# A four-layer graph network on one core: node counts fetched and compared inside the first dense layer, half of one stage's norms ended by ScalarE

## The chip, the cores and the metric

One Trainium2 chip, one core. The metric is the device time of one execution in microseconds (us). Before the change it is 3164.61 us, the median of 21 runs (3158.17 to 3174.01).

The engines are named as in the profile: PE (TensorE matmuls), PEld (its weight loads), DVE (VectorE), ACT (ScalarE), POOL (GpSimd) and SP (SyncE, which here only issues DMAs). Each engine works through its own list of instructions in order; an instruction that waits holds up all behind it on that engine. DMAs are issued from SP, ACT or POOL; indirect ones (gathers by a list of row numbers) from POOL.

## What is computed

A graph of 6250 nodes with 128 features and 106250 edges (100000 of two directions and one loop per node), sorted by destination `dst`. Four layers follow one another, each ended by a residual and a LayerNorm:

```python
x = layernorm(x + L0(x, edge_attr_128, src, dst, ...))   # sum of edge features by node, two dense products
x = layernorm(x + L1(x, edge_index, ...))                 # sum of x[src] by dst, two dense products, two batch norms
x = layernorm(x + L2(x, edge_index, ...))                 # twice: mean of x[src] by dst, dense products
x = layernorm(x + L3(x, edge_index, edge_attr_16, ...))   # attention over the edges of a node
...
def _layernorm(x, axis=-1, eps=1e-05):
    m = jnp.mean(x, axis=axis, keepdims=True)
    v = jnp.var(x, axis=axis, keepdims=True)
    return (x - m) / jnp.sqrt(v + eps)
```

L2 needs for every node the number of its edges (`cnt`, for the mean), and L3 the place of a node's first and last edge in the sorted list. Both follow from `upto`: for each node, how many edges have a destination up to it.

## The kernel before, in words

Nodes are worked on in 50 blocks of 125 (`PB`, `NB5`), and blocks in 13 `CHUNKS` of four (the last has two).

**Dense layers.** The sum of `x[src]` by `dst` in L1 and both sums of L2 are made by `neighbours`. For the first 5000 nodes it is a dense product with a matrix of edge counts, which the L0 stage has written to DRAM (`matrix`): 10 sums of 500 nodes, each from 10 pieces of 5 blocks. A piece (`piece`, L843, 640 KB, issued by SP) feeds 15 matmuls (L846), for each of its five blocks three: the rows of x stand in `arena` as three bf16 parts, `hi`, `mid` and `lo`, that `split` makes (ACT L377, DVE L378, ACT L379, DVE L380). So a dense layer has 100 pieces and 1500 of these matmuls. For the other nodes the edges are gathered: 16 quads of up to 12 rows-tiles (`row`, L801, one indirect DMA of POOL for 128 edges each, 183 in all, buffers for two quads), each summed by 12 small matmuls with one-hot matrices (`both`, L341), copied by ACT (L343), transposed by PE (L345) and added by DVE (L348). Below, "the first quad" to "the sixteenth" are these. A sum that is done goes through `take` (DVE L910 in L1), and the work of `then` or `late` follows a few pieces later on PE (in L1: `hidden`, L903).

**What goes on beside the first dense layer.** After each piece `each(i)` takes one step of two generators. `logits` fetches the 16 edge features (`eat`, L692, L694, cleared by L691, seven buffers) and multiplies them on DVE (L684, L685). `counting` finds for each node block the edge `n0` from which its 128 destinations are to be read: POOL writes a row of numbers (L543), DVE compares it seven times (L545, L547), PE sums (L537), DVE makes `n0` and `n0i` (L431, L432, L540), five blocks a step, eleven steps (`i % 7 == 1`).

**After the first dense layer.** `counted` fetches for all 50 blocks at once the 128 destinations from `n0i` on (`edges_from`, L437, 50 indirect DMAs of POOL into `nd`, 25.6 KB per partition). Then come the two dense products of L1 with batch norm (L903, L941, L945, L946), and the norm stage, chunk by chunk:

- DVE L957, ACT L959, DVE L960: batch norm's scale and shift, relu, residual;
- PE L315: four transposes to nodes (`node_p`, in PSUM);
- one step of `counted` (`degrees.send`): DVE compares the chunk's fetched destinations with the node numbers (L564), sums them (L565) and adds `n0` (L566): `upto`;
- `layernorm`: DVE statistics (L291, L293), ACT square root (L295), DVE reciprocal (L298), and the norm itself, one DVE instruction per block (L300);
- SP stores the chunk to `table` (L271), `split` makes the three parts, PE L308 and ACT L309 go back to features.

After the last chunk two shifted matmuls (L575, L576) give the start of each node, the counts' reciprocal and the last edge (L577 to L580). Then the second dense layer begins: POOL fetches its rows from the stored table, SP its pieces.

The order of the generators says when steps are emitted, but not where they end up: a scheduler orders each engine's instructions by priorities and its own estimate of what is ready, and pools give buffers and with them waits. Memory of a pool that is closed is reused by the next, which then waits until it is free; `nd` is held until the last chunk of the norm stage.

Of the kernel before, what the change touches and what calls it, by code (L numbers as in the profile page):

```python
# [209 lines left out]
def by_windows(ctx: ExitStack, tc: tile.TileContext, a: dict, out: bass.AP, consts, ix):  # L210
# [70 lines left out]
    def layernorm(to, x):  # L281

        for _ in norm_steps(to, x):
            pass

    def norm_steps(to, x):
# [11 lines left out]
        nc.vector.reciprocal(rstd[:PB, :nb], sd[:PB, :nb])  # L298
        for j in range(nb):
            nc.vector.tensor_scalar(to[:, j, :], x[:, j, :], mv[:PB, j, 0:1], rstd[:PB, j:j + 1],  # L300
                                    op0=OP.subtract, op1=OP.mult)
# [248 lines left out]
    def counted(pool):  # L550
# [6 lines left out]
        nd = pool.tile([128, NB5, 128], I32, name="nd")  # L557
        edges_from(a["dst"], n0i[:PB], nd[:PB])
        for blocks in CHUNKS:
            work = yield  # L560
            cs, nb = slice(blocks[0], blocks[-1] + 1), len(blocks)
            up = upto[:PB, 1 + cs.start:1 + cs.stop]
            lt = work.tile([128, 4, F], F32, name="rest")
            nc.vector.tensor_tensor(lt[:PB, :nb], nd[:PB, cs], over(thn[:PB, cs], 128), op=OP.is_lt)  # L564
            nc.vector.tensor_reduce(up, lt[:PB, :nb], AX.X, OP.add)  # L565
            nc.vector.tensor_add(up, up, n0[:PB, cs])  # L566

# [5 lines left out]
        p = (yield).tile([128, 4, F], F32, name="node_p")[:, 0, :]  # L573
        start = p[:PB, 0:NB5]
# [6 lines left out]
        yield  # L581
# [287 lines left out]
    with tc.tile_pool(name="l1", bufs=1) as wp:  # L869
# [37 lines left out]
        with tc.tile_pool(name="l1d", bufs=1) as dp, tc.tile_pool(name="l1e", bufs=7) as two, \  # L907
                tc.tile_pool(name="hps", bufs=4, space=bass.MemoryType.PSUM) as hps:
# [7 lines left out]
            logit, indices = logits(dp, two), counting(dp, hps)  # L916

            def each(i):
                if i % 7 == 1:
                    next(indices, None)  # L920
                if i % 3 == 2:
                    next(logit, None)

            neighbours(None, take, then, tables[0], len(matrix), each)
            for x in (logit, indices):
                for _ in x:
                    pass
        counts = ExitStack()
        degrees = counted(counts.enter_context(tc.tile_pool(name="l1c", bufs=1)))
        next(degrees)  # L930
        with tc.tile_pool(name="l1p", bufs=1) as lp, tc.tile_pool(name="l1w", bufs=2) as work, \
# [4 lines left out]
            for k in range(len(PARTS)):  # L936
# [11 lines left out]
                if k in (2, 4):  # L948
                    next(looped)
        batchnorm(2, s2, b2, g2, be2)  # L950
        with tc.tile_pool(name="l1x", bufs=2) as work, tc.tile_pool(name="zps", bufs=3, space=bass.MemoryType.PSUM) as zps, \
                tc.tile_pool(name="tps", bufs=2, space=bass.MemoryType.PSUM) as tp:
            last = None
            for blocks in CHUNKS:
# [9 lines left out]
                degrees.send(work)  # L964
                layernorm(xn[:PB, b0:b0 + nb, :], z)
# [6 lines left out]
            degrees.send(zps)  # L972
        counts.close()
# [950 lines left out]
```

## Time and profile before

| what | number |
|---|---|
| median of 21 runs | 3164.61 us (3158.17 to 3174.01) |
| the profiled execution | 3168.92 us, its span 3167.1 us |
| busy share of the span | PE 79%, DVE 55%, POOL 53%, PEld 48%, ACT 28% |
| granted PE clock, mean | 0.899 |
| first dense layer, first to last sum | 641.4 to 1006.5 us |
| norm stage of L1, DVE | from 1060.8 to 1139 us |
| first row of the second dense layer, its first and last sum | 1141.2, 1151.2, 1525 us |

The profile is of one execution. For every instruction it has the start, the length, the line of the code and what ended the idle time before it. Groups are written as line, engine, operation, out<-in and count. A view of windows gives the busy time of each engine in a stretch, with the share of full speed at which PE's clock was granted. In the timeline, the bracket behind an instruction says how long its engine had been idle before it and what came last before it went on; "issue" is time in which it waited for nothing that the profile shows.

### The profile page before, as it was taken

Reading aid. Unit: us, or ns where it says so; the run is one execution under the profiler, and the core shown is the slowest. Engines: PE = TensorE matmul, PEld = TensorE weight load, DVE = VectorE, ACT = ScalarE, POOL = GpSimd, SP = SyncE. Lnnn points to the kernel's source line nnn. Section 1 sums busy time; section 2 is a strip of 40 time slices with the busy share of each in tenths; the row PEclk is TensorE's granted clock in tenths of the full one; section 3 lists DMA queues with packets and bytes.
Section 4 is the critical chain, followed back from the end, with each engine's and each line's share of the span. In section 5 each row is a group of like instructions: output and inputs, shape, how many; then the busy total and the mean of one; then the engine's idle time right before and its main releaser. Section 6 shows DMA issues by size and latency. Waiting matters only on the chain.

```text
span 3167.1 us, 42839 instructions
## 1 busy us (share of the span) xinstructions
PE 2511.8 (79%) x14960; PEld 1532.5 (48%) x14960; DVE 1728.5 (55%) x4636; ACT 898.3 (28%) x1661; POOL 1673.9 (53%) x1664
## 2 busy tenths in 40 slices
PE   2788899989999669999999999276666666766665
PEld 1444445634444334545544444165555555655564
DVE  4777874569512850000131112477767777877776
ACT  0688884400001410000210000033323332333332
POOL 5000002078742546665077742577777777777773
PEclk9998889989999779999999999588888888988888
DMA  5799972188773256666376665322222222222221
GB/s 159 228 308 299 301 257 93 46 248 257 228 217 111 69 169 200 198 195 185 88 251 189 212 187 163 79 63 70 69 67 71 66 71 70 71 69 69 70 69 39
DMA packets 335096, 465.22 MB, mean 147 GB/s; under 512 B 45340, under 2 KB 219196, under 8 KB 334275
## 3 DMA queue, kind: packets, MB, share of 16 engines
q1 hardware_dynamic: 251434, 278.98, 29.9%
q0 software_dynamic: 54912, 105.86, 12.4%
q10 hardware_dynamic: 28524, 77.55, 6.7%
q8 instruction: 119, 1.95, 0.3%
q14 instruction: 107, 0.88, 0.1%
HBM read 377.01 MB, written 85.06 MB: 146 GB/s over the span
## 4 chain that ended last, share of the span: by engine, by line
PE 32%; DVE 13%; DMA 8%; issue 6%; POOL 6%; ACT 3%; DVEq 0%; ACTq 0%; POOLq 0%; SPq 0%
PE sums L846 16%; PE o L1203 6%; DMA rows<-x,srca 5%; POOL rows L1093 4%; DVE w L1191 3%; DVE w L1176 2%; ACT w L1193 2%; POOL row L801 2%; PE yp L1021 1%; PE w_p L1181 1%; DMA row<-table,srca 1%; DVE mx L1184 1%; PE fp L1137 1%; PE o L1153 1%; PE both L341 1%
## 5 line engine op out<-in xcount | busy, mean ns | idle before, releaser
L846 PE MATMUL sums<-piece,arena 125*128 125x500 bf16 x4500 | 990.4, 376 | 4.3 <-DMA piece<-edges 4.3
L1093 POOL DMA_INDIRECT rows<-x,srca x831 | 843.5, 1015 | 278.1 <-issue 171.8
L801 POOL DMA_INDIRECT row<-table,srca x549 | 540.8, 985 | 292.6 <-issue 128.2
L846 PEld LDWEIGHTS <-arena 125*128 125x128 bf16 x4500 | 431.2, 97 | 518.0 <-issue 33.2
L1203 PE MATMUL o<-rows,w 128*120 128x132 f32 x2078 | 359.6, 313 | 240.7 <-ACT w L1193 240.7
L1203 PEld LDWEIGHTS o<-rows,w 128*120 128x120 f32 x2078 | 309.4, 211 | 283.7 <-ACT w L1193 283.4
L646 ACT CAST arena<-made 128x1000 bf16<-128x1000 f32 (+1 forms) x260 | 315.9, 1280 | 61.9 <-PE made L644 57.5
L1193 ACT ACTIVATE w<-w 128x720 f32<-128x720 f32 x208 | 167.0, 803 | 438.0 <-DVE w L1191 399.7
L644 PE MATMUL made<-okey,olow 128*128 128x250 bf16 x1000 | 258.1, 400 | 35.2 <-ACT arena L646 17.2
L1181 PE MATMUL w_p<-ident,w 128*120 128x128 f32 x1248 | 200.0, 296 | 23.4 <-DVE w L1176 21.1
L1184 DVE TENSOR_REDUCE mx<-w_p 120x1 f32<-120x768 f32 x208 | 197.7, 951 | 18.8 <-PE w_p L1181 17.8
L343 ACT COPY by_node<-both 128x128 f32<-128x128 f32 (+1 forms) x48 | 12.7, 264 | 684.9 <-PE both L341 627.5
L352 DVE TENSOR_TENSOR onehot<-iota,relg 128x384 f32<-128x384 f32 x118 | 63.8, 545 | 247.1 <-PE both L341 235.4
L1176 DVE TENSOR_TENSOR w<-oh,z 128x720 f32<-128x720 f32 x208 | 187.3, 901 | 8.2 <-PE o L1203 6.6
L717 POOL MEMSET ea<- 128x128 f32 x1 | 0.2, 206 | 357.1 <-DMA ea<-in_edge_attr_dram 357.1
L1191 DVE TENSOR_TENSOR w<-w,both 128x720 f32<-128x720 f32 x208 | 186.8, 898 | 2.8 <-PE both L1188 2.4
L1181 PEld LDWEIGHTS w_p<-ident,w 128*120 128x120 f32 x1248 | 159.4, 150 | 54.2 <-DVE w L1176 23.1
L644 PEld LDWEIGHTS <-olow 128*128 128x128 bf16 x1000 | 109.9, 119 | 155.3 <-issue 69.4
L617 DVE TENSOR_TENSOR okey<-iok,key 128x1000 bf16<-128x1000 bf16 (+1 forms) x260 | 169.9, 653 | 0.0
L348 DVE TENSOR_TENSOR arena<-arena,both 128x32 f32 x183 | 34.2, 187 | 211.4 <-PE both L345 203.2
L1161 DVE TENSOR_TENSOR z<-rows,zed 128x12 f32<-128x12 f32 x208 | 34.4, 165 | 197.0 <-DMA rows<-x,srca 196.7
L341 PE MATMUL sums<-ea,onehot 128*32 128x128 f32 x1662 | 98.6, 335 | 47.6 <-DMA ea<-in_edge_attr_dram 30.4
(287 smaller groups left out, 3362.1 us busy)
## 6 DMA issues: line engine op xcount, KB each, us to landing
piece<-edges SPq DMA_DIRECT2D x300, 625.0 KB
edges<-arena ACTq DMA_DIRECT2D x100, 625.0 KB
ea<-in_edge_attr_dram SPq DMA_DIRECT2D x69, 768.0 KB
loop<-x SPq DMA_DIRECT2D x208, 68.0 KB
rows<-x,srca POOLq DMA_INDIRECT x831
row<-table,srca POOLq DMA_INDIRECT x549
eat<-in_edge_attr_dram POOLq DMA_DIRECT2D x28, 236.0 KB
table<-xn SPq DMA_DIRECT2D x24, 224.0 KB
```

The lines of the kernel that those rows point to most:

```text
L617: nc.vector.tensor_tensor(o[:, :, 0:n], numbers[:, :, 0:n], of.rearrange("p (o g) -> p o g", o=1).to_broadcast([128, m, n]), op=OP.is_equal)
L644: nc.tensor.matmul(p[:, i, 0:NB5 * GD], lhsT=o[:, :, i], rhs=w[:, :, i], start=True, stop=True)
L646: nc.scalar.copy(to, p[:, 0:n, 0:NB5 * GD].rearrange("p i (h d) -> p i h d", d=GD))
L801: nc.gpsimd.indirect_dma_start(out=r[:, j, :], out_offset=None, in_=table, in_offset=bass.IndirectOffsetOnAxis(ap=ix["src"][:, t:t + 1], a ...
L846: nc.tensor.matmul(p, lhsT=xp[:PB, h, i, :], rhs=t[:PB, :, (h - h0) * SC:(h - h0 + 1) * SC], start=(h == 0 and i == 0), stop=(h == NB5 - 1 ...
L1093: nc.gpsimd.indirect_dma_start(out=r[:, j, :], out_offset=None, in_=x3, in_offset=bass.IndirectOffsetOnAxis(ap=ix["src"][:, BT * b + j:BT ...
L1176: nc.vector.tensor_tensor(w, oh.to_broadcast([128, S, H, BW]), z.rearrange("p j (h w) -> p j h w", w=1).to_broadcast([128, S, H, BW]), op= ...
L1181: nc.tensor.transpose(tp[:, j // 3, j % 3 * 128:(j % 3 + 1) * 128], w[:, j, :, :].rearrange("p h w -> p (h w)"), ident)
L1184: nc.vector.tensor_reduce(mx, tp[:, :, 0:384], AX.XY, OP.max)
L1191: nc.vector.tensor_tensor(wf, wf, mb.rearrange("p (j h) w -> p j (h w)", j=1) .to_broadcast([128, S, H * BW]), op=OP.subtract)
L1193: nc.scalar.activation(wf, wf, AF.Exp)
L1203: nc.tensor.matmul(o[:, 0:F + H + 1], lhsT=wf[:, j, :], rhs=rr, start=(j == 0), stop=(j == S - 1))
```

## The change

Two edits.

1. `counted` becomes a generator within the first dense layer. It fetches the destinations for two blocks at a time into one of three small buffers (`nd` of 1 KB per partition) and compares the two blocks before, on DVE, with the result in bf16. `each` steps it twice per piece from piece 72 of 100 on. The fetches are kept in program order among the instructions so marked. `counting` steps every sixth piece instead of every seventh. The end of it, the shifted matmuls and what follows from them, becomes `degrees`, called within the second of the dense products of L1. Nothing of it remains in the norm stage.
2. In the norm stage, two blocks of each chunk get their norm from ACT instead of DVE: `Identity` with scale `rstd` and bias `off` = -mean * rstd, which DVE makes for the chunk in one small instruction.

```diff
     def norm_steps(to, x, by_act=0):
...
         nc.vector.reciprocal(rstd[:PB, :nb], sd[:PB, :nb])
+        if by_act:
+            off = small.tile([128, 4], F32, name="off")
+            nc.vector.scalar_tensor_tensor(off[:PB, :nb], mv[:PB, :nb, 0], -1.0, rstd[:PB, :nb],
+                                           op0=OP.mult, op1=OP.mult)
         for j in range(nb):
+            if j < by_act:
+                nc.scalar.activation(to[:, j, :], x[:, j, :], AF.Identity, bias=off[:PB, j:j + 1],
+                                     scale=rstd[:PB, j:j + 1])
+                continue
             nc.vector.tensor_scalar(to[:, j, :], x[:, j, :], mv[:PB, j, 0:1], rstd[:PB, j:j + 1],
                                     op0=OP.subtract, op1=OP.mult)
...
-    def counted(pool):
+    def counted(pool, work):
...
-        nd = pool.tile([128, NB5, 128], I32, name="nd")
-        edges_from(a["dst"], n0i[:PB], nd[:PB])
-        for blocks in CHUNKS:
-            work = yield
+        found = []
+
+        def compare(blocks, nd):
             cs, nb = slice(blocks[0], blocks[-1] + 1), len(blocks)
             up = upto[:PB, 1 + cs.start:1 + cs.stop]
-            lt = work.tile([128, 4, F], F32, name="rest")
-            nc.vector.tensor_tensor(lt[:PB, :nb], nd[:PB, cs], over(thn[:PB, cs], 128), op=OP.is_lt)
+            lt = pool.tile([128, 2, 128], BF16, name="fewer")
+            nc.vector.tensor_tensor(lt[:PB, :nb], nd[:PB, :nb], over(thn[:PB, cs], 128), op=OP.is_lt)
             nc.vector.tensor_reduce(up, lt[:PB, :nb], AX.X, OP.add)
             nc.vector.tensor_add(up, up, n0[:PB, cs])
+
+        for blocks in [c[i:i + 2] for c in CHUNKS for i in (0, 2) if c[i:]]:
+            nd = work.tile([128, 2, 128], I32, name="nd")
+            for i, b in enumerate(blocks):
+                tc.keep_in_program_order(nc.gpsimd.indirect_dma_start(
+                    out=nd[:PB, i, :], out_offset=None, in_=a["dst"].rearrange("(e o) -> e o", o=1),
+                    in_offset=bass.IndirectOffsetOnAxis(ap=n0i[:PB, b:b + 1], axis=0)))
+            yield
+            found.append((blocks, nd))
+            if len(found) > 1:
+                compare(*found.pop(0))
+        compare(*found.pop(0))
+
+    def degrees(pool, psum):
...
-        p = (yield).tile([128, 4, F], F32, name="node_p")[:, 0, :]
-        start = p[:PB, 0:NB5]
+        start = psum.tile([128, 2 * SC], F32, name="hp2")[:PB, 0:NB5]
...
+                tc.tile_pool(name="l1n", bufs=3) as ndp, \
...
+            finding = counted(dp, ndp)
             def each(i):
-                if i % 7 == 1:
+                if i % 6 == 1:
                     next(indices, None)
                 if i % 3 == 2:
                     next(logit, None)
+                if i >= 72:
+                    next(finding, None)
+                    next(finding, None)
...
-        counts = ExitStack()
-        degrees = counted(counts.enter_context(tc.tile_pool(name="l1c", bufs=1)))
-        next(degrees)
...
+                if k == 6:
+                    degrees(lp, hps)
...
-                degrees.send(work)
-                layernorm(xn[:PB, b0:b0 + nb, :], z)
+                layernorm(xn[:PB, b0:b0 + nb, :], z, 2)
...
-            degrees.send(zps)
-        counts.close()
```

More of the change, by code (lines that the diff above doesn't have):

```diff
@@ L279, in row_over, with layernorm, norm_steps @@
         return x.rearrange("p (b f) -> p b f", b=1).to_broadcast([PB, nb, x.shape[1]])
-    def layernorm(to, x):
-        for _ in norm_steps(to, x):
+    def layernorm(to, x, by_act=0):
+        for _ in norm_steps(to, x, by_act):
             pass
-    def norm_steps(to, x):
+    def norm_steps(to, x, by_act=0):
         nb = x.shape[1]
@@ L580, in counted @@
         nc.vector.tensor_scalar(lasti[:PB], upto[:PB, 1:], -1.0, None, op0=OP.add)
-        yield
     def products():
@@ L922, in each @@
                     next(logit, None)
+                if i >= 72:
+                    next(finding, None)
+                    next(finding, None)
             neighbours(None, take, then, tables[0], len(matrix), each)
-            for x in (logit, indices):
+            for x in (logit, indices, finding):
                 for _ in x:
                     pass
-        counts = ExitStack()
-        degrees = counted(counts.enter_context(tc.tile_pool(name="l1c", bufs=1)))
-        next(degrees)
         with tc.tile_pool(name="l1p", bufs=1) as lp, tc.tile_pool(name="l1w", bufs=2) as work, \
```

## The prediction

> **What bounds the kernel now.** I read the page first (busy shares by slice), then the windows around the change, then the chain of waits from 620 to 1180 us, then POOL's and PE's instructions in order of time. The stages touched are the first dense layer (641 to 1006), the two dense products of L1 (1006 to 1061), the L1 norm stage (1061 to 1138) and the start of the second dense layer (to 1151). The table of windows gives, per stretch, length, then busy us of PE, PEld, DVE, ACT and POOL, the granted PE clock, DMA share and GB/s:
>
> ```profile
> 632.00:870.00 238.00, 218.99 (x1245) 101.90 (x1249) 176.80 (x283) 2.65 (x10) 186.72 (x210) 0.96 0.79 244
> 870.00:1006.00 136.00, 136.00 (x730) 62.74 (x723) 17.85 (x55) 1.58 (x6) 37.79 (x39) 1.00 0.60 185
> 1061.00:1138.00 77.00, 31.62 (x104) 21.05 (x104) 76.02 (x253) 32.63 (x63) 20.96 (x17) 0.51 0.21 54
> 1151.00:1525.00 374.00, 374.00 (x2005) 183.62 (x2004) 35.32 (x107) 27.53 (x60) 230.13 (x226) 1.00 0.66 199
> ```
>
> The dense layers are PE's: it is busy all the time from 870 to 1006 and from 1151 to 1525. The norm stage is DVE's: 76 of 77 us. In 632 to 870 POOL looks free (187 of 238), and is not. Its timeline (start, length, instruction, idle before it) shows that every indirect fetch is followed by 0.30 us in which nothing is waited for:
>
> ```profile
> 858.82 0.94 POOL L801 DMA_INDIRECT row<-table,srca  x1 [0.30 <-issue]
> 860.07 0.94 POOL L801 DMA_INDIRECT row<-table,srca  x1 [0.30 <-issue]
> 861.32 0.99 POOL L801 DMA_INDIRECT row<-table,srca  x1 [0.30 <-DMA row<-table,srca]
> 862.61 1.50 POOL L801 DMA_INDIRECT row<-table,srca  x1 [0.30 <-issue]
> ```
>
> So a row costs POOL 1.25 us. Adding up the gaps beyond that 0.30 from 634 to 880 leaves under 4 us: until about 870 POOL is full. After it POOL waits for free row buffers, and idles from 935.
>
> What moves is this group (min/median/max ns, first and last start), and what it feeds on DVE:
>
> ```profile
> L437 POOL DMA_INDIRECT nd<-in_dst_dram,n0i x50: 1178/1197/2340, 1007.0 to 1083.9; - x50
> L564 DVE TENSOR_TENSOR rest<-nd,node_col x13: 418/685/693, 1038.0 to 1134.8; 125x512 f32<-125x512 int32 x12, 125x256 f32<-125x256 int32 x1
> ```
>
> A fetch costs POOL 1.197 + 0.30 = 1.50 us.
>
> **First dense layer: +40.** The edit asks for the fetches from piece 72 of 100 on, where POOL is idle. But the order in which the changed kernel, as built, hands POOL its instructions puts them earlier: 5 fetches stand ahead of the fourth quad's rows, 8 ahead of the fifth's, 18 ahead of the eighth's, 30 ahead of the ninth's, 35 ahead of the tenth's, 40 ahead of the twelfth's, and only 10 behind the last. POOL works in that order, and PE's order has the quads' matmuls at the same pieces as before, so a late quad stops PE and all sums behind it. In before the twelfth quad's last row is issued by 869.7 and its matmuls run at 891.4 to 892.0:
>
> ```profile
> L341 PE MATMUL both<-row,onehot x24: 272/273/297, 891.4 to 892.0; 128*32 128x128 f32 x24
> ```
>
> 40 x 1.50 = 60.0 us more ahead of it, and landing: in the third layer, where PE does wait for rows, a quad's last matmul starts 1.9 us after its last row's issue ends (1685.1, 1687.0). 869.7 + 60.0 + 1.9 = 931.6 against 892.0: late by 39.6. The ninth quad (817.6 + 45 + 1.9 against 831.0) is late by 33.5 already, the eighth (802.5 + 27 + 1.9 against 814.2) by 17; from the thirteenth on POOL gains on PE (15 us of rows per 17 to 22 us of PE), so 40 stays. Lower end: the 4 us of POOL's idle absorb as much, and contention does not lengthen the fetches: 34. Upper end: rows in this stretch run at up to 1.5 us instead of 0.94 here and there; fetches at 1.6, and waits for DVE: 50. DVE's 25 compares of two blocks (0.42 + 0.42 + 0.15 = 0.99 each, from the 256-wide rows: 24.7 us) lie in its 61 idle us of 632 to 870; but a compare waits in DVE's order for its fetch, with one-hots, L348 and `take` behind it, and a fetch waits for a compare three tiles back. As ordered, the fourth `take` stands behind the thirteenth compare, thus behind POOL's eighth quad and 8 more fetches, and PE's `hidden` of that sum stands ahead of the eighth quad's matmuls: 802.5 + 27 + 13 (8 fetches and a chunk of `eat`) + 2 to land + 5 of DVE's work between puts it near 850, and PE needs 19 us from there to the ninth quad: 869 against 830.4, again 39. Where DVE is full (59 of 60 us in 700 to 760) that cover is gone; this is in the upper end.
>
> **The two products: 0.** One chunk's compare (1.5 us at 1038) leaves DVE, `degrees` comes (four matmuls of 50 columns, 0.9 us on DVE).
>
> **Norm stage: -12.5.** Off DVE: L564, L565 and L566 of 11.5 chunks, which start 0.69 + 0.60 + 0.13 apart: 16.3; two of four L300 of each chunk, 26 x 0.32 = 8.3; the closing L577 to L580, 1.0. On it: `off`, 13 x 0.15 (as L566) = 2.0. DVE's floor is 77 - 23.6: one end is -23.6. The other is 0: two other engines take over. ACT gets 26 norms; nearest rows are its 128x128 copy (L343, 0.26) and the 125x256 cast (0.40): I take 0.35, 9 us, ACT 42, not the bound. PE gets new work: the big `nd` tile gone, the second layer's pieces find room before the stage ends, and PE's order now has about 148 of that layer's 1500 sums among the transposes, some 125 ahead of the last chunk's. A late chunk's transposes stand behind sums that read the split of about two chunks earlier. Priced from before: a chunk's chain from its first statistics to its split took 10.9 us (1125.4 to 1136.3) on a full DVE; less the 1.9 that each of two chunks no longer takes: 7.1; transposes 1.3 and ten sums of 0.211: 10.5 per two chunks, 5.2 per chunk, 65 for 12.5 chunks. 77.5 - 65 = 12.5, between the ends.
>
> **Second dense layer: -25.** The first row is fetched when the last table rows have landed, and PE then waits for rows, not sums:
>
> ```profile
> 1141.21 0.98 POOL L801 DMA_INDIRECT row<-table,srca  x1 [54.68 <-DMA l2wr<-in_L_gnn_W_r_dram]
> ...
> 1150.66 0.63 PE L341 MATMUL both<-row,onehot 128*32 128x128 f32 x2 [2.69 <-DMA row<-table,srca]
> ```
> ```profile
> L341 PE MATMUL both<-row,onehot x24: 272/273/297, 1215.7 to 1216.3; 128*32 128x128 f32 x24
> ```
>
> Counted from that first row, the third quad's matmuls came at +74.5. In the new order the first two quads stand at pieces 11 to 14, and the sums ahead are done in time: the second quad's rows are issued by +30.2, landed by +32.1; then 45 sums (9.5) and the first mean's products (7.5: the 23.3 us between these quads before, less 75 sums) give +49.1. The third quad's rows (by +46.7, landed 48.6) don't delay it. Gain 25.4. From there POOL needs some 19 us a quad, PE 22: nothing is lost again. Ends: -28, and -18 if rows land as late as the 5.6 us at 1145.
>
> **Sum**, on the profiled execution: 3168.92 us with a span of 3167.1 and 1.8 around it. +39.6 + 0 - 12.5 - 25.4 = +1.7. That execution is 4.3 above the median of 21 runs, 3164.61, so I forecast 3166.3, call it 3167: no change. 0.2% (6.3 us) is about what a measurement here can tell from none.
>
> [...] The clock: PE's granted clock was 0.51 in the norm stage and came back some 3 us after its sums ran without gaps (from 1151.2 they started 0.42 apart, later 0.211). [...] Also, half of the norms change from a copy-like form to Identity with pointers. A table load took 1.28 us where Exp and Sqrt alternate after 2046. [...]
>
> **Rivals.**
> - *Slower: the norm stage keeps its length.* At half clock 125 sums take 52 us and 100 transposes 27 (50 x 0.32 + 50 x 0.21, this stage's spacing): 79, no less than 77.5. From about 65 us of PE work on, PE is the bound. For: clock 0.51 now. Against: runs of 6, 12 and 15 sums stand together. Price 12.5: 3179. A table load before each Sqrt and Identity group (26 x 1.28 = 33 on ACT, 75 in all) would give the same; the change would then not do what it says for DVE. With it I count a longer stall of the first layer (50: 3177). 0.36.
> - *Faster: DVE's floor is reached and POOL absorbs its 4 us.* 36 - 23.6 - 25.4 = -13: 3152. For: the as-built order interleaves two to three chunks. Against: the sums between transposes. If the fetches cost PE nothing at all, 3167 - 40 = 3127; the gapless POOL timeline speaks against it (0.04). Together 0.26.
> - *No change*, 0.38.
>
> **Range.** Best ends 34 - 23.6 - 28 = -17.6; worst 50 - 0 - 18 = +32. Both at once are unlikely; 8 in 10: 3150 to 3187. Faster by over 0.2% 0.26, within 0.38, slower 0.36.
>
> **What would show it.** Right: `nd` fetches from about 700 on between rows; PE idle before the eighth and ninth quads' matmuls on `row`, some 35 us together; the last sum of the first layer near 1046; norm stage of 60 to 68 us with PE's sums inside; the third quad of the second layer some 49 us after its first row. Wrong: no such idle in the first layer (much faster), or the norm stage still 77 us long (slower).

## The result and the profile after

The changed kernel takes **3219.07 us** (median of 8 runs, 3212.74 to 3220.76) against 3166.53 (56 runs) for the kernel before: ratio 1.016, 95% interval 1.0148 to 1.0172, that is 52 us slower. The forecast was 3167, with a range up to 3187; the time lies outside it. The profiled execution of the changed kernel took 3216.04 with a span of 3214.2, 47.1 more than before.

By stage, between the same instructions in both traces (L1 is the first dense layer, from its first sum to its last; the products run from there to the last `bnshift`; the norm stage from there to the first row of the second layer; the second layer from that row to the third layer's first sum):

| stage | before | after | difference | forecast |
|---|---|---|---|---|
| L1 | 364.8 | 457.2 | **+92.4** | +39.6 (34 to 50) |
| two products | 54.4 | 54.7 | +0.3 | 0 |
| norm stage | 80.7 | 62.3 | -18.4 | -12.5 (-23.6 to 0) |
| second layer from its first row | 443.7 | 420.6 | -23.1 | -25.4 (-28 to -18) |
| start, third layer, rest | 2223.5 | 2219.4 | -4.1 | 0 |

So the norm stage and the second layer came out inside their bounds and the products at 0.3. The miss is L1, 52.8 us above its term. The windows of the changed kernel, in the columns of the table of windows of before (length, busy us of PE, PEld, DVE, ACT, POOL, granted clock, DMA share, GB/s):

```profile
632.00:870.00 238.00, 171.29 (x909) 78.40 (x913) 155.65 (x271) 1.86 (x7) 183.94 (x199) 0.86 0.66 200
870.00:1098.20 228.20, 202.29 (x1067) 92.72 (x1059) 60.61 (x157) 2.39 (x9) 104.99 (x101) 0.93 0.55 170
1153.00:1215.20 62.20, 54.41 (x260) 29.44 (x261) 56.00 (x203) 42.70 (x92) 0.05 (x1) 0.89 0.48 137
1215.20:1602.40 387.20, 375.79 (x1980) 184.12 (x1979) 41.17 (x117) 33.89 (x70) 236.01 (x233) 0.98 0.61 183
```

From 632 to 870 PE did 909 matmuls where it had done 1245. DVE and POOL were *less* busy than before (156 against 177, 184 against 187) although both had been given work: PE and DVE waited. POOL did not: counted with the 0.30 us behind every indirect fetch, it had some 8 us of other idle time in this stretch (3 before), so that it was as full as the prediction had it. In the norm stage the granted clock is 0.89, not 0.51, and PE has 260 matmuls there instead of 104.

The moved fetches and their compares (min/median/max ns, first and last start):

```profile
L578 POOL DMA_INDIRECT nd<-in_dst_dram,n0i x50: 1178/1199/2055, 698.2 to 1029.0; - x50
```
```profile
L571 DVE TENSOR_TENSOR fewer<-nd,node_col x25: 411/425/426, 703.8 to 1032.9; 125x256 bf16<-125x256 int32 x25
```

Both cost what the prediction took (1.197 and 0.42), and the fetches begin where it said. What PE waited for in L1, before and then after (us in all, times, longest). The wait for a row in the first list is the one ahead of the very first sum; the changed kernel has it too (9.9 us), just outside the stretch of its list.

```profile
PE both L341 <- DMA row<-table,srca: 10.3, 1, 10.3
PE both L341 <- DVE arena L348: 10.2, 4, 7.6
```
```profile
PE both L349 <- DVE arena L356: 84.2, 9, 26.0
```

And what DVE waited for, after:

```profile
DVE fewer L571 <- DMA nd<-in_dst_dram,n0i: 81.9, 19, 15.2
DVE below L553 <- POOL arena L551: 39.9, 5, 23.4
DVE onehot L360 <- PE both L349: 38.7, 7, 9.7
DVE arena L356 <- PE both L353: 30.8, 5, 11.0
```

Apart from that first row, PE does not wait for rows at all. In every quad from the third on, the last row had been issued 22 us or more before the quad's last matmul. All of PE's idle time ends with L356, DVE's addition of a quad's transposed sums, and most of DVE's idle time ends with an `nd` fetch. Not all of either is the change: 8.5 us of PE's 84.2 lie ahead of the first `nd` fetch (7.6 at the same place before), and so do 23.4 of the 39.9 us that DVE waits for L551, the iota of a counting step, called the ramp below (22.1 before). The longest of these stalls, on POOL, then DVE, then PE (start, length, instruction, idle before it):

```profile
816.95 1.58 POOL L578 DMA_INDIRECT nd<-in_dst_dram,n0i  x1 [0.30 <-DVE upto L572]
818.84 1.19 POOL L578 DMA_INDIRECT nd<-in_dst_dram,n0i  x1 [0.31 <-issue]
820.34 0.98 POOL L820 DMA_INDIRECT row<-table,srca  x1 [0.30 <-issue]
...
834.64 0.95 POOL L820 DMA_INDIRECT row<-table,srca  x1 [0.30 <-issue]
835.60 0.68 POOL L551 IOTA arena<- 119x625 f32 x1
836.46 1.20 POOL L578 DMA_INDIRECT nd<-in_dst_dram,n0i  x1 [0.19 <-issue]
837.97 1.20 POOL L578 DMA_INDIRECT nd<-in_dst_dram,n0i  x1 [0.31 <-issue]
```
```profile
825.04 0.18 DVE L356 TENSOR_TENSOR arena<-arena,both 128x32 f32 x1
825.15 0.16 DVE L573 TENSOR_TENSOR upto<-upto,n 125x2 f32<-125x2 f32 x1
825.23 0.68 DVE L703 TENSOR_TENSOR product<-eat,veb 119x512 f32<-119x512 f32 x1
825.84 0.18 DVE L356 TENSOR_TENSOR arena<-arena,both 128x32 f32 x1
841.25 0.43 DVE L571 TENSOR_TENSOR fewer<-nd,node_col 125x256 bf16<-125x256 int32 x1 [15.24 <-DMA nd<-in_dst_dram,n0i]
841.60 0.18 DVE L356 TENSOR_TENSOR arena<-arena,both 128x32 f32 x1
```
```profile
841.83 1.51 PE L349 MATMUL both<-row,onehot 128*32 128x128 f32 x24 [26.04 <-DVE arena L356]
```

Read together: DVE did the earlier additions of a quad, the third at 825.84, and came to a compare that stands between them and the fourth. Its two destinations were not fetched yet: POOL had twelve rows (the eighth quad's) and a ramp to issue first, and issued the two fetches from 836.46 to 839.17. So DVE stood for 15 us with one addition of 0.18 us to do behind the compare, and PE for 26. The rows for which DVE stood were not even the ones that PE needed next: PE's next matmuls were the seventh quad's. Another stop, of 14.3 us, ended behind a ramp: it stands in POOL's queue behind the fifth quad's rows, and DVE stood 4.8 us for it, until 749.17.

Two quads later the same thing is seen in the rows. The ninth quad's last row was issued by 874.8, 57 us later than before (817.6), and its matmuls came 69 us later than before, still 24 us after that row:

```profile
873.86 0.94 POOL L820 DMA_INDIRECT row<-table,srca  x1 [0.30 <-issue]
```
```profile
899.02 1.51 PE L349 MATMUL both<-row,onehot 128*32 128x128 f32 x24 [10.66 <-DVE arena L356]
```

Clock: in the changed kernel eight of the nine stops behind L356 cost a second time, by a granted clock of 0.50 that sets in during the stop or within 1.4 us of its end; the one of 2.9 us (until 715.9) did not. Around the longest stop:

```profile
820.00:847.00 27.00, 5.17 (x34) 2.33 (x35) 8.84 (x21) 0.27 (x1) 21.43 (x23) 0.50 0.18 48
847.00:869.00 22.00, 19.53 (x92) 8.90 (x90) 18.63 (x40) 0.00 (x0) 15.92 (x14) 0.99 0.68 205
```

In this one, PE stood for most of the 27 us at half clock and worked for 5 of them. Over L1 the mean granted clock fell from 0.98 to 0.90, and PE's busy time for the same 1966 matmuls rose from 354.5 to 373.1. So the 92 us are 74 of added idle time and 18 of lost clock.

The second layer went as forecast; its third quad, 50.8 us after the first row at 1215.2 (forecast 49.1, before 74.5):

```profile
L349 PE MATMUL both<-row,onehot x24: 272/273/297, 1266.0 to 1266.6; 128*32 128x128 f32 x24
```

### The profile page after: what moved, and what is told of

Its sections match the earlier page's. It is cut to its first block, busy times and chain, and to the rows that moved or that the text cites. A ratio compares the mean times of both kernels' runs of the same rounds, so it can differ in the third digit from the quotient of the medians.

```text
span 3214.2 us, 42912 instructions
## 1 busy us (share of the span) xinstructions
PE 2513.3 (78%) x14960; PEld 1518.5 (47%) x14960; DVE 1723.3 (54%) x4659; ACT 907.4 (28%) x1687; POOL 1670.5 (52%) x1664
## 4 chain that ended last, share of the span: by engine, by line
PE 51%; DVE 17%; DMA 12%; issue 7%; POOL 7%; ACT 6%; DVEq 1%; SPq 0%; ACTq 0%; POOLq 0%
PE sums L865 23%; PE o L1223 6%; DMA rows<-x,srca 5%; PE made L663 5%; DVE w L1211 3%; POOL rows L1113 3%; DVE w L1196 3%; ACT arena L665 3%; POOL row L820 3%; ACT w L1213 2%; PE sums L349 2%; DMA row<-table,srca 2%; PE yp L1041 1%; PE hp L776 1%; PE yp L783 1%
## 5 line engine op out<-in xcount | busy, mean ns | idle before, releaser
L865 PE MATMUL sums<-piece,arena 125*128 125x500 bf16 x4500 | 1014.9, 381 | 7.6 <-DMA piece<-edges 4.3
L1223 PE MATMUL o<-rows,w 128*120 128x132 f32 x2078 | 352.2, 308 | 247.1 <-ACT w L1213 247.1
L1223 PEld LDWEIGHTS o<-rows,w 128*120 128x120 f32 x2078 | 301.5, 207 | 290.7 <-ACT w L1213 290.3
L1201 PEld LDWEIGHTS w_p<-ident,w 128*120 128x120 f32 x1248 | 158.3, 150 | 56.2 <-DVE w L1196 25.4
L349 PE MATMUL both<-row,onehot 128*32 128x128 f32 x1098 | 55.8, 303 | 122.0 <-DVE arena L356 84.2
L356 DVE TENSOR_TENSOR arena<-arena,both 128x32 f32 x183 | 34.1, 186 | 198.4 <-PE both L353 190.8
```

Source lines behind the costliest of these rows:

```text
L865: nc.tensor.matmul(p, lhsT=xp[:PB, h, i, :], rhs=t[:PB, :, (h - h0) * SC:(h - h0 + 1) * SC], start=(h == 0 and i == 0), stop=(h == NB5 - 1 ...
L1201: nc.tensor.transpose(tp[:, j // 3, j % 3 * 128:(j % 3 + 1) * 128], w[:, j, :, :].rearrange("p h w -> p (h w)"), ident)
L1223: nc.tensor.matmul(o[:, 0:F + H + 1], lhsT=wf[:, j, :], rhs=rr, start=(j == 0), stop=(j == S - 1))
```

## The experiments

Runs were made in five sets, each on another chip: the first four below, the next four, the next four, then three, then two. On the chips of the first, third, fourth and fifth set the kernel before took 3499.89, 3503.79, 3533.62 and 3500.91 us, against 3166.02 in the second, and the ratios below are against the kernel before on the same chip; the layers with indirect fetches and the last stage were longer there for every kernel (from the second layer's first row to the end 2351 us in the run of the norms alone, 2026 in the trace of the kernel before), and PE shows short gaps amid sums that nothing explains (15 in L1 of the run of the norms alone, 11.0 us in all; none in L1 of the kernel before). On such a chip L1 of the kernel before is taken as 377.9, from the run of the norms alone, which leaves L1 as it was; "loss" below is L1 against 364.8 (second set) or 377.9 (the others). Stages are read from one profiled execution of each kernel, so that differences of 2 or 3 us say nothing. No kernel leaves out work of the network; what it does more, or elsewhere, its diff shows.

**Which part of the change costs.** First the fetches and compares without the norms, and the norms without the fetches.

In the changed kernel:

```diff
-                layernorm(xn[:PB, b0:b0 + nb, :], z, 2)
+                layernorm(xn[:PB, b0:b0 + nb, :], z)
```

> The changed kernel with all norms back on VectorE: what is left is the fetch and the comparison of the destinations in the first dense layer. Ring theory (VectorE stands at compares whose fetches POOL has not issued yet, with L356 behind them, and PE stands at the next quad): the first dense layer stays at 457 us, as in the changed kernel, 92 over the kernel before. The norms on ScalarE are worth 26 x 0.32 - 2.0 = 6.3 us if VectorE bounds the norm stage: stage 62.2 + 6 = 68 us, time 3225. Rival, that another engine bounds the stage in the new order: stage 62, time 3219. If the norms were the cause of the loss, the time would fall to the kernel before's 3166 or below.

Measured: 1.0167 (1.0139 to 1.0196); L1 461.2, loss 83; norm stage 67.8. The loss is the fetches and compares alone. The norms on ScalarE are worth 5.5 us of stage (67.8 against 62.3), near the 6.3 worked out.

And in the kernel before, with `norm_steps` of the changed kernel:

```diff
-                layernorm(xn[:PB, b0:b0 + nb, :], z)
+                layernorm(xn[:PB, b0:b0 + nb, :], z, 2)
```

> The kernel before with two of four norms of each chunk ended by ScalarE, nothing else. First dense layer 365 us, unchanged, under every theory. Norm stage: VectorE is busy 77.4 of 80.5 us there; less 26 x 0.32, plus 13 x 0.15, it would be 74: time 3160. Rival, PE and the chain of a chunk set the stage: no change, 3166. Table loads on ScalarE would make it slower by up to 33 us: 3199.

Measured: 0.9985 (0.9968 to 1.0001); norm stage 73.6 against 80.7. The stage gains what VectorE is spared; the time can't be told from no change.

**POOL's time without waits for it.** The kernel before with fifty more fetches that nothing reads, beside its own:

```diff
+        for blocks in [c[i:i + 2] for c in CHUNKS for i in (0, 2) if c[i:]]:
+            nd = work.tile([128, 2, 128], I32, name="spare")
+            for i, b in enumerate(blocks):
+                tc.keep_in_program_order(nc.gpsimd.indirect_dma_start(
+                    out=nd[:PB, i, :], out_offset=None, in_=a["dst"].rearrange("(e o) -> e o", o=1),
+                    in_offset=bass.IndirectOffsetOnAxis(ap=n0i[:PB, b:b + 1], axis=0)))
+            yield
...
-                if i % 7 == 1:
+                if i % 6 == 1:
+                if i >= 72:
+                    next(finding, None)
+                    next(finding, None)
```

> The kernel before, which still fetches and counts at its old place, with 50 more fetches of the same destinations in the first dense layer into a tile that nothing reads; in POOL's order 25, 30, 35 and 40 of them stand ahead of the eighth, ninth, tenth and twelfth quad's rows, as in the changed kernel. It holds POOL's time alone. Queue theory (that of the prediction: 40 x 1.50 us of POOL make rows late): first dense layer 365 + 40 = 405 us, PE's idle before L349's like named as the rows' transfers, time 3206. Ring theory: POOL's time is part of the loss at most, the layer is 365 to 405 us long, and the 52 us beyond 405 of the changed kernel are not here.

Measured: 1.0192 (1.0157 to 1.0228); L1 446.2, loss 68, between the theories. PE did not wait for rows here either (each quad's last was issued 9.5 us or more ahead): 21.6 us of its waits end with VectorE's `take`, and VectorE waited for the ramp L543, the counting steps' iota, which stands behind the fetches in POOL's queue. Both theories had overlooked that wait:

```profile
DVE below L545 <- POOL arena L543: 51.3, 3, 29.1
DVE below L545 <- issue: 42.1, 3, 23.4
```

The waits of the second line also end 0.03 us after a ramp, so that it is 93 us in all, against 30 in the kernel before and 22 in the run of the norms alone on this chip.

To these, compares of a tile that is long there are added:

```diff
+            lt = pool.tile([128, 2, 128], BF16, name="spare_lt")
+            nc.vector.tensor_tensor(lt[:PB, :nb], over(n0i[:PB, cs], 128), over(thn[:PB, cs], 128), op=OP.is_lt)
+            nc.vector.tensor_reduce(up2[:PB, cs], lt[:PB, :nb], AX.X, OP.add)
+            nc.vector.tensor_add(up2[:PB, cs], up2[:PB, cs], n0[:PB, cs])
```

> As the spare fetches, with 25 compares, reductions and additions more on VectorE, of the same shapes and at the same places, whose input is not the fetched tile but one that is long there; results go to a spare tile. It holds POOL's time and VectorE's work without the wait between them. Ring theory: close to the spare fetches alone, first dense layer at most 415 us. Load theory (25 us of compares on a VectorE that is full until 870): 457 us as in the changed kernel, time 3258 as the old fetches are still there too. Queue theory: 405.

Measured: 1.0252 (1.0223 to 1.028); L1 458.6, loss 81: against the ring theory as it stood, which had the loss go with the compares' wait. So POOL's lateness is handed on by the ramp too, or VectorE's work does cost.

**The same work behind the rows.**

The changed kernel, with every `nd` fetch bound behind the row fetch that the text issued last:

```diff
-                        nc.gpsimd.indirect_dma_start(
+                        last_row = nc.gpsimd.indirect_dma_start(
                             out=r[:, j, :], out_offset=None, in_=table,
...
-                tc.keep_in_program_order(nc.gpsimd.indirect_dma_start(
+                with tc.issue_after(last_row.ins):
+                    nc.gpsimd.indirect_dma_start(
...
-                if i >= 72:
+                if i >= 84:
```

> The changed kernel with one thing more: each fetch of destinations is bound behind the last row fetch that the text has issued so far, and they begin at piece 84 instead of 72, so that in POOL's order all 50 stand behind the last row of the sixteenth quad, and all 25 compares behind its one-hots. Order theory (the loss is POOL's 60 us ahead of rows and ramps, handed on by VectorE's order): the first dense layer is as in the kernel before, plus at most 10 us, because the last `take` stands behind compares whose fetches end about 75 us after the last row (935 + 75 = 1010 against the last sum at 1006). Norm stage and second layer keep their gains of 18 and 23: 31 to 41 us faster than the kernel before. Rival, that the extra work of the first layer costs wherever it stands (40 fetches' contention and 25 us of VectorE): first layer 40 or more longer, no faster than before.

Measured: 1.0034 (1.0022 to 1.0046); L1 415.4, loss 51, norm stage 61.6. No fetch stands ahead of any row, and each quad's last row was issued some 13 us or more ahead of the quad's last matmul, yet PE stopped:

```profile
PE both L349 <- DVE arena L356: 50.9, 6, 24.3
```
```profile
DVE fewer L571 <- DMA nd<-in_dst_dram,n0i: 50.5, 23, 10.2
```

So compares that wait cost by themselves, in VectorE's order. The expectation's "at most 10" was wrong: the bound was on POOL alone.

> As the last one, but begun at piece 72 as in the changed kernel: 20 fetches stand ahead of the fifteenth quad's rows and 40 ahead of the sixteenth's, none ahead of the fourteenth's. By POOL's times of the kernel before: rows of the fifteenth end at 924 + 30 = 954 against 947, those of the sixteenth at 935 + 60 = 995 against 969. Queue theory: first layer 26 us longer, in all some 15 us faster than the kernel before. Order theory with VectorE's waits: up to 50 longer, no gain. If what counts is only the number of fetches ahead of the ninth quad: 0 to 5 longer, 35 us faster than the kernel before.

(The same with 72 for 84.) Measured: 1.0101 (1.0079 to 1.0123); L1 437.7, loss 73, more than any theory gave; 74.7 of PE's idle time ends with L356.

The spare fetches with one ramp:

```diff
+        nc.gpsimd.iota(row, pattern=[[1, M * PB]], base=1, channel_multiplier=0,
+                       allow_small_or_imprecise_dtypes=True)
+        dfc = pool.tile([RB, RT], F32, name="dfc")
         for c in range(steps + 1):
...
-                nc.gpsimd.iota(row, pattern=[[1, M * PB]], base=c * M * PB + 1, channel_multiplier=0,
-                               allow_small_or_imprecise_dtypes=True)
+                nc.vector.tensor_scalar(dfc, ix["df"][:, 0:RT], float(-c * M * PB), None, op0=OP.add)
...
```

(The compares that follow read `dfc` in place of `ix["df"]`.)

> The spare fetches again, with the ramp that the counting compares against (POOL's iota in each of its ten steps) made once, ahead of the layer; each step moves the thresholds instead, by one small VectorE instruction of some 0.15 us. With it the only thing left for which VectorE's order waits on POOL in this layer is `eat` and the one-hots' buffers. In the spare fetches the layer was 68 us longer than without them, and VectorE waited 51 us for that ramp. Theory that the lateness is handed on at the ramp: the layer gets 15 to 35 us shorter than with the spare fetches, down to the queue theory's +40 or less. Theory that rows or row buffers hand it on: no more than 5 us shorter.

Measured: 1.0114 (1.0092 to 1.0136); L1 405.6, loss **41**. This is the forecast's picture: from the seventh to the ninth quad the last row is issued 1.8 to 3.5 us before its last matmul, and PE stops for it, one row after the other:

```profile
PE both L341 <- DVE arena L348: 18.7, 4, 12.8
PE both L341 <- DMA row<-table,srca: 16.4, 11, 3.6
```

So where VectorE waits for POOL neither at ramps nor at compares, late rows stop PE as the forecast had it, and the size is near its 39.6. In part that is luck: only 26 of these 41 are added idle time, and 14 are clock (granted 0.94 for 0.98, busy 368.8 for 354.5), which the forecast had not counted, and the run counts by six, which the next one shows to cost 11.

> The kernel before with the counting steps at every sixth piece instead of every seventh, nothing else. Every theory so far has this at no cost: first layer as before within 5 us, time within 0.2%. If the layer is 10 us or more longer, part of what was put down to the fetches is this.

(`i % 7` to `i % 6` in the kernel before.) Measured: 1.0035 (1.0021 to 1.0048); L1 376.1, loss **11.3**. A part of the change that the prediction gave no cost: PE's waits for L348 rose from 10.2 to 18.2 us.

**VectorE's order.** The run behind the rows, with the text's order on VectorE too (`mark` holds the last L356, one-hots, `take` or `bn_stats` of the text), counting by seven again, one pair of fetches a piece, and the pairs that are left in the products. The diff is against the changed kernel; the fetches are bound as in the run behind the rows:

```diff
-                if i % 6 == 1:
+                if i % 7 == 1:
...
-                if i >= 72:
-                    next(finding, None)
-                    next(finding, None)
+                if i >= 84:
+                    next(finding, None)
...
-                compare(*found.pop(0))
+                with tc.issue_after(mark[0].ins):
+                    compare(*found.pop(0))
...
                 if k in (2, 4):
                     next(looped)
-                if k == 6:
+                if k < 11:
+                    next(finding, None)
+                if k == 11:
                     degrees(lp, hps)
```

> The changed kernel with the same work in another order: counting every seventh piece again; from piece 84 on one pair of fetches a piece, bound behind the last row fetch on POOL; each pair's compares bound on VectorE behind the last instruction of the dense layer that was issued before them, instead of where the order put them; the 11 pairs that are left then go with the parts of the two dense products, and the starts and degrees come at part 11. Order theory: no row, no ramp and no L356 stands behind a fetch, so that the first layer is 365 us as in the kernel before, the products 55, norm stage 62 and second layer 421 from its first row as in the changed kernel: 41 us faster than the kernel before, 3125. If the extra work of the first layer costs by itself (VectorE's 25 us, contention of fetches): 3145 or more. If compares that wait for fetches hold the products up: the products 65 to 75 us, 3140.

Measured: **0.9942** (0.9922 to 0.9961), faster than both kernels. L1 380.4, loss 2.5. The layer does not hold the same work, though: 33 of the 50 fetches and 14 of the 25 compares fall into it, the others into the products. These took 65.5, 11 more: 7.8 us of it PE's wait for the degrees' first matmul, behind the last compare. L1 and the products together lose 13.6 us here (445.9 against 432.3 in the run of the norms alone), where the same fetches and compares in the built order lost 84 (515.9, first run, which counts by six). The second layer took 497.7 against 507.8 in the run of the norms alone, less of a gain than the 23 us on the other chip. The longer products and this are the main reasons why 22 us were gained and not 41.

> As the last one, but the compares are not bound on VectorE: in the order as built all 25 stand ahead of the last `take` and 17 of them ahead of the fifteenth quad's last L356, while POOL's order is as in the last one. It tells VectorE's waits apart from everything else. Order theory: VectorE stands at compares for fetches that take 3.1 us a pair, L356 and PE's next quad behind them: first layer 25 to 45 us longer than in the last one (the fetches alone need 75 us from 935 to 1010, the last quad's L356 comes after some 22 pairs: 935 + 68 = 1003 against 960). Rival: compares are ready when they are reached, within 5 us of the last one.

(Without the two `issue_after(mark...)`.) Measured: 1.0024 (1.0002 to 1.0046); L1 421.0, 40.6 more than with them. First this one's waits of PE in L1, then those of the run before it:

```profile
PE both L351 <- DVE arena L358: 36.2, 2, 26.2
PE sums L872 <- issue: 11.3, 15, 1.5
```
```profile
PE sums L874 <- issue: 7.2, 6, 2.4
PE both L351 <- issue: 6.2, 13, 1.0
```

POOL's queue has no fetch ahead of any row in either; what differs is the place of the compares on VectorE. Free, they go ahead of the last quads' additions. Sixteen of them stand between those of the fourteenth and of the fifteenth quad, each waiting for its pair of fetches, and PE stands for the fifteenth's (VectorE, then PE):

```profile
977.33 0.41 DVE L358 TENSOR_TENSOR arena<-arena,both 128x32 f32 x2
978.41 0.43 DVE L573 TENSOR_TENSOR fewer<-nd,node_col 125x256 bf16<-125x256 int32 x1 [0.66 <-DMA nd<-in_dst_dram,n0i]
...
1023.40 0.43 DVE L573 TENSOR_TENSOR fewer<-nd,node_col 125x256 bf16<-125x256 int32 x1 [1.48 <-DMA nd<-in_dst_dram,n0i]
1024.60 0.19 DVE L358 TENSOR_TENSOR arena<-arena,both 128x32 f32 x1 [0.78 <-issue]
```
```profile
1027.16 1.49 PE L351 MATMUL both<-row,onehot 128*32 128x128 f32 x6 [26.23 <-DVE arena L358]
```

The waits do this, and not the compares' work: in step, compares that need not wait follow one another in 0.99 us, and sixteen of these would have been done by 994 (an estimate), ahead of PE, which stopped at 1000.9. So the waits are worth 36 us of PE's idle time. The 41 us of L1 hold something else too, because free all 25 compares and 50 fetches fall into L1; L1 and the products together are 476.1 free and 445.9 in step, 30 us apart.

> The changed kernel with the counting steps at every seventh piece again, nothing else. If the costs add, the first layer is 11 us shorter than in the changed kernel (the counting by six cost 11.3 alone): 446 us, 3203. If the fetches' lateness hides it: 457, 3214.

(`i % 6` to `i % 7` in the changed kernel.) Measured: 1.0117 (1.0082 to 1.0152); L1 453.8 against 461.2, 7 less, 11 expected; PE's gaps amid sums are 21 us here and 9 there, so between 7 and 20. With the two runs before it, on the same chip and with the same counting, it gives the worth of the order for L1 and the products together: 508.4 as built, 476.1 with the fetches behind the rows, 445.9 with the compares in step too. Of the first step, 16 us are gaps that nothing explains.

> The changed kernel with the counting ramp made once ahead of the layer, as in the spare fetches with one ramp. VectorE then waits in this layer on POOL at the compares alone. If ramp and compares hand POOL's lateness on in turn: 10 to 28 us shorter than the changed kernel, 430 to 447 us. If the compares alone do it: 457. If the compares cost nothing once the ramp is gone: 406 as in the spare fetches with one ramp.

(The one ramp in the changed kernel.) Measured: 1.0163 (1.0129 to 1.0196); L1 456.9, 4 less: with compares that wait, the ramp hardly matters. VectorE waited 75.0 us at compares.

**Is it the waits or the work?**

> The spare fetches and the spare compares (which don't wait for them) together, with the counting ramp made once. So POOL's 40 fetches stand ahead of the rows and VectorE has its 25 compares more, but VectorE's order waits for POOL neither at a ramp nor at a compare. With the ramp in each step and compares that don't wait the loss was 81 us; with one ramp and compares that wait 79; with one ramp and no compares 41. Theory that either wait hands POOL's lateness on by itself, and VectorE's work costs little: 405 to 420 us for the first layer on a chip where it is 365 before, loss 41 to 55. Load theory: loss about 80 again.

(Spare fetches, spare compares and one ramp.) Measured: 1.0218 (1.0195 to 1.0241); L1 451.3, loss 73. Not settled by the number: rows are late as in the run with one ramp (issued 1.7 to 1.8 us ahead of the seventh to ninth quad's last matmuls), but 25.7 us of PE's time went into gaps amid sums (11.0 in the run of norms alone), and VectorE stood 15 us for the last spare fetch, which gave PE a stop of 9. Without these, 50 is left (73.4 - 14.7 - 8.9), in the range of the waiting theory. The gaps were not understood, and L1 of the kernel before was not measured on this chip, so that this subtraction is an estimate. So it stays open what 25 compares cost by their work alone at the places where the built order put them.

> The in-step order, begun at piece 78 instead of 84: 6 fetches then stand ahead of the sixteenth quad's rows (34 us early), 20 pairs go with the dense layer, and 5 instead of 11 with the products, the degrees at part 6. If the products were 11 us longer because of pairs of 3.1 us in each part: products 55 to 58, the rest as in the in-step order: 7 to 11 us faster than it, 1.2% faster than the kernel before. If the products wait for the degrees: still 65.

Measured: **0.9935** (0.9922 to 0.9947), L1 391.8, products 55.1, norm stage 62.2. The products are back, so their 11 us had been the 11 pairs left over; but L1 lost as much (391.8 for 380.4; ten compares stand among the last quads' L356 instead of four, and the gaps amid sums are 12.6 us for 7.2), and the time can't be told from the run in step. With 20 of the 25 compares and 45 of the 50 fetches in L1, none of PE's idle time there ends with VectorE, and the loss is 14.

> The spare fetches (unread, ramp in each step) on the same chip as the two above, because chips differed by 10% in the stages of indirect fetches. Theory that the ramp hands the lateness on: first layer 15 to 35 us longer than the 406 us with one ramp, if this is a chip like that one. If the difference between the two runs was the chip's: within 5 us of it.

Measured once: L1 446.4, as in the first set (446.2). So the 68 is no accident of that run. With one ramp and the spare compares (the first run of this set) it was 451.3.

> The kernel before with the counting ramp made once ahead of the layer and the thresholds moved in each step, nothing else. Theory that the ramp only hands on lateness that POOL has from the fetches: no gain here, first layer 360 to 366 us on a chip where it is 365, time within 0.2%. Rival, that the ramp is a cost of its own wherever it stands (VectorE waits 30 us for it in the kernel before too): 10 to 15 us shorter.

Measured: 1.0007 (0.9988 to 1.0027), L1 380.2 (377.9 without). The ramp is no cost of its own; its waits cost where POOL is late.

> The in-step order begun at piece 78, with one ramp. If the ramp costs only where POOL is late, the same as without it within 5 us: 22 to 30 us faster than the kernel before. If it is a cost of its own: 10 to 15 us more than that.

Measured: 0.9939 (0.9916 to 0.9963), L1 390.1: no more than without it.

## Why the prediction was wrong, point by point

- **First dense layer, +39.6: the step that failed.** The prediction found two ways from POOL's delay to PE: late rows, and a `take` behind a compare that waits. It worked out 39 for each and took them as one ("again 39"), with the compares' work hidden in VectorE's idle time. That step failed: the path through VectorE was not one place that falls together with late rows. Compares at the places of the built order cost PE 36 us of idle time, and 30 to 41 us of time, with no fetch ahead of a row (in step, free against bound), and counting by six, which had no price, cost 11. POOL's time alone costs 41 where VectorE does not wait for it (spare fetches with one ramp, which count by six as well).
- **How it went in the changed kernel.** Until 870 it is a chain from POOL's full queue. A compare waits for a fetch that stands behind the twelve rows of a later quad, L356 stands behind the compare, and PE waits for L356. So PE came to wait for POOL's work ahead of the rows that it needed next, and these lay ready for 22 us or more; the ninth quad's rows were 57 us late, its matmuls 69. From 870 on the chain closes to a ring: rows wait some 24 us for buffers that PE frees, and the last ten fetches stand behind them. The fetch's own wait for a compare three tiles back, which the prediction names, held POOL for 0.6 us in all.
- The prediction saw the links and wrote that a compare stands ahead of one-hots, L348 and `take`; it priced only the worst single place instead of following the order from compare to compare. The places were there to see: 16 of 25 compares stand ahead of the tenth quad's one-hots.
- **Clock in L1: not counted.** 18 of the 92 us. The prediction weighed the clock for the norm stage, where it feared it, and not in the layer whose PE it made idle. PE worked for 45 us at half clock there, against 7.5 before. The eight half-clock stretches (granted clock 0.50) that begin in L1 of the changed kernel last 3.4, 6.8, 10.2, 13.7 and 27.3 us, in this trace multiples of 3.4, and their starts (686.8, 741.5, 796.1, 820.0, 871.2, 891.6, 929.2 and 1031.6) lie whole multiples of 3.41 us apart, 101 of them from the first to the last.
- **What the 92 are made of can't be added up term by term.** Rows 41 and compares' waits 30 to 41 were measured apart, on chips that differ, the first holds the counting by six, and ramp or compare wait can each stand in for the other (waits at ramps alone 81, at compares alone 79, at both 83). What is shown: with the same fetches and compares and the counting by seven, on one chip, order takes L1 and the products from 508.4 to 445.9 us, 13.6 above the run of the norms alone (on another chip). What VectorE's work would cost without any wait stays open: some 14 us or less where 20 compares stand late in the layer (in step from piece 78), not known where they stand early.
- **Two products, 0:** right, 0.3. **Second layer, -25.4:** right, 23.1, by the mechanism given: the third quad came 50.8 us after the first row.
- **Norm stage, -12.5:** right in sign, sized too small: 18.4, inside its bounds. The norms on ScalarE are 5.5 of it (the run of counts only against the changed kernel) and 7.1 alone; which part of a chunk's chain was shorter than the 5.2 us was not tested. The rival that PE at half clock would bound the stage was wrong: the clock was 0.55 from 1153 to 1168 and 1.00 from there to 1215 (0.51 before), where the second layer's sums themselves fill PE. The prediction had counted half clock against the change in this stage; after the first 15 us there was none:

```profile
1153.00:1168.00 15.00, 10.46 (x34) 6.60 (x35) 13.25 (x53) 8.69 (x19) 0.00 (x0) 0.55 0.14 35
1168.00:1215.00 47.00, 43.75 (x227) 22.75 (x226) 42.75 (x151) 34.01 (x74) 0.00 (x0) 1.00 0.59 169
```

- **Norms on ScalarE:** 0.46 us each, not 0.35, and no table load between Sqrt (L295) and Identity (L305): none stands among the 13 of the one and the 26 of the other in this stage, where the rival had counted 26 of 1.28 us. ScalarE's timeline (start, length, idle before it):

```profile
1158.56 0.30 ACT L295 ACTIVATE sd<-mv,epst 125x4 f32<-125x4 f32 x1 [0.37 <-DVE mv L293]
1159.41 0.81 ACT L305 ACTIVATE xn<-node_p,off,rstd 125x128 f32<-125x128 f32 x2 [0.55 <-DVE off L301]
1160.11 0.29 ACT L295 ACTIVATE sd<-mv,epst 125x4 f32<-125x4 f32 x1
```

- **Signs:** fetches from 698 and the norm stage of 62 us came as named. Idle time on `row` (35 us) and the last sum near 1046 did not: the idle time is 84 us, all on L356, and the last sum came at 1098. The slower rival had the right side with the wrong mechanism; its "longer stall of the first layer" ended at 50.

## What to carry to other kernels

A fetch and its use that move into a busy stage bring two orders, not one: the queue that fetches, and the engine that uses. On the using engine each use was a gate for everything behind it (here a compare that waited 15.2 us, with an addition of 0.18 us behind it, held PE for 26.0), so follow what stands behind each one in the order as built, and give these waits a price of their own unless a run shows that they hide behind the fetcher's delay. Slack in the data (rows 22 us early here) protected nothing where the stop came through another engine's queue. When the work fits into idle time but the layer grows, bind the order on both engines before giving the idea up: here, on one chip, that turned 1.2% slower (counting by seven) into 0.6% faster.

## What the runs showed of the hardware that was not expected

- A stop of PE of 26 us (815.8 to 841.8) brought a granted clock of 0.50 from 820.0 to 847.3. PE worked for only 5 us of that, so that one long stop cost little clock; the nine half-clock stretches of L1 (two before) together cost 18 us.
- Chips differ by stage: between the second set's chip and the others the two products took the same (54.4 us), the second layer from its first row 444.8 against 501 to 516 in kernels of the old fetch place, and what follows the third layer 1182 against 1367 to 1407. The mean length of a row fetch on POOL in L1 hardly differs (1.024 us in the trace of the kernel before, 1.027 in the run of the norms alone, whose L1 is the same), so it is not the issue of fetches there; what it is stays open.
